# An attention and convolution kernel: whole products gathered in every other region, conv steps between them

## The chip, the cores and the metric

The kernel runs on one core of a Trainium2 chip. The metric is the time on the device from start to end in microseconds (us), median of three runs: 3374.07 us before the change (3363.94 to 3385.05).

## The reference, cut to what matters

Two layers on four images of 128 channels and 128 x 128 pixels, in float32.

Layer 0 is region attention with a conv network behind it:

```python
reg = x[:, :, ih, iw]                       # 9 x 9 regions of 16 x 16 pixels, step 14, so 2 overlap
tok = reg as (b * 81, 256, 128)
q, k, v = split(layernorm(tok) @ w_qkv)     # 4 heads of 32 channels
o = softmax(q k^T / sqrt(32)) v             # per region and head, 256 x 256
tok = o @ w_out + b_out + tok
xf = (sum of the regions' tok at each pixel) / (how many regions hold the pixel)
ym = layernorm(xf) @ w_p0 + b_p0            # 256 channels
ym = depthwise_conv_5x5(ym)
ym = gelu(gelu(batchnorm(ym)))              # means over all images
x1 = ym @ w_p2 + b_p2 + xf
```

Layer 1 quantises to 4 bits, convolves 3 x 3, normalises over the batch, twice, and adds x1. It is the last part of the kernel, and the change does not touch it, except for the preparation of its two quantised weights, which runs beside the attention.

## The kernel before, in words

Channels lie on the 128 partitions. An image is cut into nine **bands** of one row of nine regions each, so there are T = 36 bands, and the main loop runs over bands t and over the nine regions j of a band. The first stage (attention and depthwise conv) ends at about 2434 us, then come `gelu_stage` and `last_stages`.

**Region work.** For each region the loop calls `scores(j)` (L663: eight matmuls in tiles of 32 rows by 128 columns, one per head and half of the keys, then two exponentials of 128 x 1024 on ScalarE), the value step of the region before (`last`, made of `values(j)`, L725: products of 128 rows by 32 columns, then the sums over the keys with a matrix of ones, then on VectorE a reciprocal and two multiplications, and on GpSimd the addition at the seam), `halves(j)` (L679: the two halves of the keys are added, one pair on GpSimd and one on VectorE) and `values_in(j)` (L653: v of the region, two whole 128 x 128 products and a copy on ScalarE).

**Side work.** Between these calls stand three lists of side steps, which `beside(t)` (L765) returns for each region. They hold
- `one`: layer norm and projection of the next band, in two chunks `a1` and `a2` of nine steps: squares, variance (matmuls with ones, tiles of 128 x 32), deviation, spread (the row of factors goes through DRAM and comes back on all partitions), second (scaling), and four q and k products of 512 or 384 columns;
- `two`: the band before, in two chunks `b1` and `b2` of eleven steps: two output projections (`wo`, L499), squares, variance, deviation, spread, second, and four products with `w_p0` (L515) whose results go to DRAM as `y2_d`;
- `conv`: steps taken from the list `todo`.

**The list todo.** It first holds the quantisation of layer 1's weights (`quantised`, L281) and the making of the conv matrices (`band_matrices`, L202, whose `turn`, L253, reorders a 40 x 2048 tile on VectorE or ScalarE). Later it gets the depthwise conv of each finished image (`conv_steps`, L545): one first step that loads, then 32 tiles per image, each with loads of u and w from DRAM, 24 matmuls in tiles of 40 rows by 32 columns, two copies on ScalarE, statistics on VectorE and stores to `cv_d` in pieces of 256 bytes. The last image is cut into a half and two quarters of 16 tiles each. `share` says how many steps a band takes, and a fixed order (0, 3, 5, 7, 1, 2, 8, 4, 6) which regions get them.

**What sets the order.** On TensorE, ScalarE, VectorE and SyncE (`MANUAL`) instructions stand in the order in which the code emits them; every engine works its queue in that order. Nearly all DMAs are issued from SyncE's queue, and a store is issued right after the step that made it (`run` and `flush`).

**Buffers.** The score tiles take four of the eight PSUM banks (one buffer of two tiles), the value tile one (`ps_o`), and three banks (`ps_m`, "pm") serve everything else: value inputs, statistics, products, conv steps. In SBUF: `xp` holds the input rows (3), `xfp` the output projection (1), `xnp` the scaled rows (3), `y2p` two buffers per half for the y stores, `attn_t` the small attention tiles and v (3).

**The tail.** After band 36 the region pools are closed, `beside(T)` gives the post chain of the last band with conv steps of the third unit between, and the last quarter image runs with all its weights in SBUF (`all_w`), loaded from GpSimd's queue.

## Time and profile before

| what | us |
|---|---|
| time, median of three runs | 3374.07 |
| span of the profiled execution | 3381.3 |
| start, to the first scores | 35.4 |
| band 0 | 52.5 |
| bands 1 to 9 (no conv steps; the matrices are made) | 501.0 |
| bands 10 to 27 (conv of images 0 and 1) | 1080.6 |
| bands 28 to 32 (conv of image 2) | 376.1 |
| bands 33 and 34 (conv of a half of image 3) | 170.6 |
| band 35 and the tail | 217.9 |
| gelu and last stages | 946.9 |

A stretch ends where the scores of the next band start, read from the start times of the score matmuls, nine regions to a band. The mean granted TensorE clock over the span is 0.960 of full speed. Busy times of TensorE take in modelled ends of pipelined matmuls, so 93% busy does not mean 93% of its peak; distances between starts are the safer measure. A float32 matmul of the program stands as two records in the trace.

### The profile page before, as it was taken

To read this page: it belongs to the slowest core of one execution; us is meant where nothing else is said; L and a number is where in the kernel's file an instruction comes from. 1 tells how busy PE (TensorE), PEld (TensorE's weight loads), DVE (VectorE), ACT (ScalarE), POOL (GpSimd) and SP (SyncE) were. 2 spreads that over 40 slices of the span, in tenths; PEclk is the share of its full clock that TensorE was granted. 3 is DMA by queue.
4 is the path that set the end of the run, shared out by engine and by line. 5 is a ranking of instruction groups with operands and counts; after the bars stand their busy time and mean duration, and the time that the engine had idled before them with its cause. 6 is when DMAs were issued, how large, how long until landed. Compare 5 with 4: busy or idle time off the path is not lost. (4 is left out here: it accounts for less than half of the span.)

```text
span 3381.3 us, 75962 instructions
## 1 busy us (share of the span) xinstructions
PE 3144.9 (93%) x30922; PEld 1584.0 (47%) x30922; DVE 2006.5 (59%) x3229; ACT 2006.7 (59%) x2818; POOL 841.9 (25%) x1060
## 2 busy tenths in 40 slices
PE   6999889999999999999999999984799999999998
PEld 3555445555454554554444445552544444444343
DVE  4767666766766666666655555551455555666543
ACT  4677667666666666666655556551267677433433
POOL 2443334333333333333322222220011111000000
PEclk8999989999999999999999999896599999999999
DMA  2455655788887788878699988877699999552298
GB/s 89 131 155 148 157 137 142 185 195 190 190 199 178 184 181 195 195 189 194 157 203 206 203 193 191 206 188 198 175 360 359 359 356 316 166 174 81 77 358 312
DMA packets 812012, 682.64 MB, mean 202 GB/s; under 512 B 581550, under 2 KB 696327, under 8 KB 811655
## 3 DMA queue, kind: packets, MB, share of 16 engines
q1 hardware_dynamic: 792071, 669.03, 72.8%
q10 hardware_dynamic: 18560, 4.72, 0.6%
q8 instruction: 247, 4.05, 0.5%
q0 software_dynamic: 1024, 3.93, 0.4%
q14 instruction: 110, 0.90, 0.1%
HBM read 410.68 MB, written 270.81 MB: 202 GB/s over the span
## 5 line engine op out<-in xcount | busy, mean ns | idle before, releaser
L751 DVE RECIPROCAL rd<-po 128x256 f32<-128x256 f32 x324 | 569.4, 1757 | 513.5 <-PE po L739 511.3
L1023 PE MATMUL pc<-q,wq 128*128 128x512 fp8e4 x3168 | 702.0, 381 | 14.4 <-DVE q L1035 14.4
L676 ACT ACTIVATE pt<-sc 128x1024 f32<-128x1024 f32 x648 | 626.2, 1019 | 96.5 <-PE sc L668 64.2
L686 POOL TENSOR_TENSOR sm<-pt 128x512 f32<-128x512 f32 x324 | 417.7, 1289 | 1064.3 <-ACT pt L676 629.7
L1023 PEld LDWEIGHTS <-wq 128*128 128x128 fp8e4 x3168 | 309.1, 98 | 417.6 <-issue 50.0
L600 PE MATMUL pm<-u,w 40*32 40x504 f32 (+5 forms) x7680 | 370.9, 497 | 48.3 <-DMA u<-y_d 33.2
L668 PE MATMUL sc<-q,kr 32*128 32x256 f32 x5184 | 402.4, 405 | 1.9 <-ACT pt L676 1.7
L731 PE MATMUL po<-pt,v 128*32 128x256 f32 x5184 | 349.9, 388 | 26.8 <-ACT v L660 16.7
L611 DVE BATCH_NORM_STATS2 st<-c 128x6 f32<-128x512 f32 (+2 forms) x384 | 175.4, 506 | 255.5 <-ACT c L607 254.7
L668 PEld LDWEIGHTS sc<-q,kr 32*128 32x128 f32 x5184 | 247.8, 185 | 150.3 <-issue 105.1
L607 ACT COPY c<-pm 128x512 f32<-128x512 f32 (+1 forms) x256 | 132.4, 562 | 288.9 <-PE pm L600 247.3
L446 PE MATMUL pm<-xn,wqkv 128*128 128x512 f32 (+1 forms) x576 | 270.2, 594 | 29.1 <-DVE xn L376 26.8
L515 PE MATMUL pm<-xn,wp 128*128 128x512 f32 (+1 forms) x576 | 259.7, 575 | 8.0 <-DVE xn L376 7.8
L656 PEld LDWEIGHTS pm<-wqkv,yr 128*128 128x128 f32 x1296 | 183.4, 194 | 177.5 <-issue 100.6
L600 PEld LDWEIGHTS pm<-u,w 40*32 40x32 f32 x7680 | 161.3, 110 | 218.4 <-issue 139.6
L1081 PE MATMUL pb<-cv,wp 128*128 128x512 f32 x512 | 232.6, 598 | 12.2 <-ACT cv L1072 12.2
L686 DVE TENSOR_TENSOR sm<-pt 128x512 f32<-128x512 f32 x324 | 228.2, 704 | 11.9 <-ACT pt L676 11.9
L520 ACT ACTIVATE y<-pm,bp 128x512 f32<-128x512 f32 (+1 forms) x288 | 180.5, 640 | 80.2 <-PE pm L515 73.8
L731 PEld LDWEIGHTS po<-pt,v 128*32 128x32 f32 x5184 | 137.1, 109 | 193.8 <-issue 47.8
L656 PE MATMUL pm<-wqkv,yr 128*128 128x128 f32 x1296 | 221.1, 294 | 1.8 <-DVE rstd L352 1.1
L739 PE MATMUL po<-sm,ones 128*32 128x256 f32 x2592 | 201.6, 381 | 8.0 <-POOL sm L686 8.0
L1031 DVE BATCH_NORM_STATS2 st<-pc 128x6 f32<-128x512 f32 x256 | 165.6, 689 | 67.3 <-PE pc L1023 67.3
(149 smaller groups left out, 3468.0 us busy)
## 6 DMA issues: line engine op xcount, KB each, us to landing
cv<-cv_d SPq DMA_DIRECT2D x64, 1024.0 KB
u<-y_d SPq DMA_DIRECT2D x224, 256.0 KB
cv_d<-c SPq DMA_DIRECT2D x192, 256.0 KB
xn<-row SPq DMA_DIRECT2D x80, 512.0 KB
y_d<-y SPq DMA_DIRECT2D x160, 256.0 KB
xfl<-xf_d SPq DMA_DIRECT2D x64, 512.0 KB
id_d<-y SPq DMA_DIRECT2D x64, 512.0 KB
idt<-id_d SPq DMA_DIRECT2D x64, 512.0 KB
```

The costliest lines, as they stand in the source:

```text
L446: nc.tensor.matmul(pm[:, : n * P], wqkv[:, m * P : (m + 1) * P], held["xn"][hh], start=True, stop=True,)
L515: nc.tensor.matmul(pm[:, : n * P], wp0[:, h, :], held["xn"][hh], start=True, stop=True)
L600: nc.tensor.matmul(pc[half][32 * q : 32 * q + 32, j, :, a:z], wt[hs, s, c0 + c, :], ut[hs, :, c, a + s - 1 : z + s - 1], start=(s == 1), s ...
L656: nc.tensor.matmul(pv[:, c, :], region(yr, j)[:, c * P : (c + 1) * P], wqkv[:, 2 * P :], start=True, stop=True)
L668: nc.tensor.matmul(sc[h // 2][:, h % 2, kc, :].rearrange("p (r c) -> p r c", c=RS), region(kr, j)[hs, kc * P : (kc + 1) * P], queries(j, h ...
L676: nc.scalar.activation(pt, sc[p], AF.Exp)
L686: add(sm, pt[:, :, 0, :], pt[:, :, 1, :], ALU.add)
L731: nc.tensor.matmul(po[hs, 0, :], v[:, kc, hs], pt[h // 2][:, h % 2, kc, :], start=(kc == 0), stop=(kc == 1),)
L739: nc.tensor.matmul(po[hs, 1, :], ones, sm[h // 2][:, h % 2, :], start=True, stop=True)
L751: nc.vector.reciprocal(rd, po[:, 1, :])
L1023: nc.tensor.matmul(pc[:, h], w[:, t, :], q1[b][:, r + dy : r + dy + RB, dx : dx + P], start=(t == 0), stop=(t == 8),)
L1081: nc.tensor.matmul(pb[:, m], wp2[:, h, :], cv[:, h, px], start=(h == 0), stop=(h == 1))
```

## The change

- **Regions.** `beside(t)` returns four lists per region. From band 10 on, all whole products (q, k, output projection, `w_p0`) stand in the even regions, together with the value inputs, and conv steps stand in the odd regions first (order 1, 3, 5, 7, 8, 4, 6, 2, 0). Up to band 9 the whole products are spread over all nine regions. The purpose is to change between whole products and tiled matmuls less often, and to give the regions more even work.
- **Values of two regions at once.** `values_in` runs in even regions and fills a tile for regions j and j + 1, with one copy on ScalarE.
- **A projection one band later.** The second half's `w_p0` steps (`b2[7:]`) are kept in `left` and run in the next band's first region. The first squares of a band's input run at the end of the band before (`early`).
- **Matrix steps.** `turn` is split into two halves, all on VectorE; the edges and rows of the matrices are single steps, one per region. The largest weight is found by a store, a load onto all partitions and a reduction in place of GpSimd's `partition_all_reduce`.
- **Shares.** The steps of an image are spread evenly over the bands left for it. The third unit (a quarter of image 3) runs wholly in band 35, up to two steps per region.
- **Tail.** Half the weights are loaded ahead, half beside the first four conv steps, from SyncE's queue; no conv step stands inside the last band's chain.
- **Buffers.** `xp` 3 to 2, `xfp` 1 to 2, `attn_t` 3 to 2, and a pool `attn_v` of 2 for the value inputs.

```diff
-        work, dev, xnp, xfp = pool("work", 1), pool("dev", 2), pool("xnp", 3), pool("xfp", 1)
+        work, dev, xnp, xfp = pool("work", 1), pool("dev", 2), pool("xnp", 3), pool("xfp", 2)
...
-        xp, yp, sums = pool("xp", 3), pool("yp", 2), pool("sums", 1)
-        att, attn_t = pool("att", 2 if safe else 4), pool("attn_t", 2 if safe else 3)
+        xp, yp, sums = pool("xp", 2), pool("yp", 2), pool("sums", 1)
+        att, attn_t, attn_v = pool("att", 2 if safe else 4), pool("attn_t", 2), pool("attn_v", 2)
...
-            def turn(c, s):
-                by_c = scratch(32 * 64)[:KD]
-                copy = nc.scalar.copy if s % 2 else nc.vector.tensor_copy
-                copy(by_c.rearrange("p (c m) -> p m c", m=32), held.pop((c, s)))
-                nc.sync.dma_start(
-                    out=dw_d[c // 16 : (c + 64) // 16, :, s, :].rearrange("k p n -> p k n"),
-                    in_=by_c.rearrange("p (k n) -> p k n", n=16 * 32),
-                )
+            def turn(c, s, half):
+                if half == 0:
+                    held["c"] = scratch(32 * 64)[:KD]
+                by_m, by_c = held[c, s], held["c"]
+                nc.vector.tensor_copy(
+                    by_c[:, half * 1024 : half * 1024 + 1024].rearrange("p (c m) -> p m c", m=32),
+                    by_m[:, :, 32 * half : 32 * half + 32],
+                )
+                if half:
+                    del held[c, s]
+                    nc.sync.dma_start(
+                        out=dw_d[c // 16 : (c + 64) // 16, :, s, :].rearrange("k p n -> p k n"),
+                        in_=by_c.rearrange("p (k n) -> p k n", n=16 * 32),
+                    )
             def several(*steps):
                 def run_all():
...
             pieces = [(c, s) for c in range(0, 2 * P, 64) for s in range(3)]
-            steps = [several(zeros, *each(edges, [(b,) for b in range(B)])), padded_taps]
-            for n in range(0, GR, 2):
-                steps.append(several(*each(by_outputs, [(ro,) for ro in range(n, n + 2)])))
-            steps += [lambda: None]
-
-            for n in range(0, len(pieces) + 2, 2):
+            steps = [zeros, *each(edges, [(b,) for b in range(B)]), padded_taps, lambda: None]
+            steps += each(by_outputs, [(ro,) for ro in range(GR)])
+            steps += [lambda: None, lambda: load(*pieces[0])]
+
+            for n, p in enumerate(pieces):
                 steps.append(
-                    several(*each(turn, pieces[max(n - 2, 0) : n]), *each(load, pieces[n : n + 2]))
-                )
+                    several(lambda p=p: turn(*p, 0), *each(load, pieces[n + 1 : n + 2]))
+                )
+                steps.append(lambda p=p: turn(*p, 1))
             return steps
         def quantised(n, w):
...
-                am = small.tile([P, 1], F32, name="am")
+                am = small.tile([P, 1], F32, name="am", bufs=2)
-                held["alpha"] = small.tile([P, 1], F32, name="alpha")
-                nc.gpsimd.partition_all_reduce(held["alpha"], am, P, bass_isa.ReduceOp.max)
+                held["row"] = row = rowp.tile([4, 256], F32, name="row")
+                store(row[0:1, :P].rearrange("a p -> p a"), am)
...
+
+            def spread():
+                row = held["row"]
+                held["am"] = dev.tile([P, 256], F32, name="rstd")[:, :P]
+                nc.sync.dma_start(out=held["am"], in_=bass.AP(row.tensor, row.offset, [[0, P], [1, P]]))
             def scales():
-                alpha = held["alpha"]
...
-                        room = tail[0] if tail and at else xfp
-                        held["xf"] = room.tile([P, LB * P], F32, name="xf")
+                        held["xf"] = xfp.tile([P, LB * P], F32, name="xf")
...
             def values_in(j):
-                pv = ps_m.tile([P, 2, P], F32, name="pm")
-                for c in range(2):
-                    nc.tensor.matmul(
-                        pv[:, c, :], region(yr, j)[:, c * P : (c + 1) * P], wqkv[:, 2 * P :], start=True, stop=True
-                    )
-                v = attn_t.tile([P, 2, P], F32, name="v")
-                nc.scalar.copy(v, pv)
-                S["v", j] = v
+
+                two = range(j, min(j + 2, NR))
+                pv = ps_m.tile([P, 2, 2, P], F32, name="pm")
+                for m in range(len(two)):
+                    for c in range(2):
+                        nc.tensor.matmul(
+                            pv[:, m, c, :], region(yr, j + m)[:, c * P : (c + 1) * P], wqkv[:, 2 * P :],
+                            start=True, stop=True,
+                        )
+                v = attn_v.tile([P, 2, 2, P], F32, name="v")
+                nc.scalar.copy(v[:, : len(two)], pv[:, : len(two)])
+                for m in range(len(two)):
+                    S["v", j + m] = v[:, m]
             def scores(j):
                 sc = [ps_s.tile([P, 2, 2, NT], F32, name=f"sc{p}") for p in range(2)]
...
-            one = ln1_chunks(t + 1) if t + 1 < T else []
+            one = list(early) if t else ln1_chunks(1)
+            early[:] = ln1_chunks(t + 2) if t + 2 < T else []
             two = post_chunks(t - 1) if t else []
+            had = len(todo)
             if t >= 2:
                 b, i = bands[t - 2]
                 if i == NR - 1 and b < B - 1:
                     todo.extend(conv_steps(b))
-                    share[0] = -(-len(todo) // (NR if b < B - 2 else 5))
+                    share[0] = NR if b < B - 2 else 5
                 elif b == B - 1 and i == 4:
                     todo.extend(conv_steps(B - 1))
-                    share[0] = NR
+                    share[0] = 2
                 elif b == B - 1 and i == 6:
                     todo.extend(conv_steps(B))
-            conv = [todo.pop(0) for _ in range(min(share[0], len(todo)))]
+                    share[0] = 1
+
+            fresh = len(todo) > had
+            n = len(todo) // share[0] if fresh else -(-len(todo) // max(share[0], 1))
+            conv = [todo.pop(0) for _ in range(n)]
+            share[0] -= 1
             a1, a2 = one if one else ([None] * 9,) * 2
             b1, b2 = two if two else ([None] * 11,) * 2
             if t == T:
-                c = conv + [None] * (9 - len(conv))
                 return [
-                    *b1[:2], *b2[:2], b1[2], b1[3], b2[2], b2[3], b1[4], b2[4], *c[:3], b1[5], b2[5],
-                    *c[3:6], b1[6], *b1[7:], b2[6], *b2[7:], *c[6:],
+                    *conv, *left, *b1[:2], *b2[:2], b1[2], b1[3], b2[2], b2[3], b1[4], b2[4], b1[5], b2[5],
+                    b1[6], *b1[7:], b2[6], *b2[7:],
                 ]
+
             c = [[] for _ in range(NR)]
-            for j in sorted((0, 3, 5, 7, 1, 2, 8, 4, 6)[: len(conv)]):
+            d = [[] for _ in range(NR)]
+            twice = len(conv) > NR
+            for j in sorted((1, 3, 5, 7, 8, 4, 6, 2, 0)[: len(conv)]):
                 c[j] = [conv.pop(0)]
+                d[j] = [conv.pop(0)] if twice and j and conv else []
             x1 = lambda: fetch(t, 0)
             x2 = lambda: fetch(t, 1)
-            return [
-                ([], [a1[0], *c[0]], []),
-                ([a1[1]], [b1[0], b1[1], *c[1]], [a1[2], b1[2]]),
-                ([b1[3]], [a1[3], *c[2]], [b1[4], a2[0]]),
-                ([a2[1]], [b1[5], *c[3]], [a1[4], a2[2]]),
-                ([], [b1[6], a2[3], a1[5], a1[6], *c[4]], [b2[0], b2[1], b2[2]]),
-                ([b2[3]], [a1[7], a1[8], *c[5]], [b2[4], a2[4], b1[7], b1[8]]),
-                ([], [b2[5], b1[9], b1[10], *c[6]], [a2[5], a2[6]]),
-                ([], [b2[6], x1, a2[7], a2[8]], c[7]),
-                ([], [x2, b2[7], b2[8], *c[8]], [b2[9], b2[10]]),
+            f, left[:] = list(left), b2[7:]
+            s1 = early[0][0] if early else None
+            plan = [
+                ([a1[1]], [], f, [*c[0], a1[2]]),
+                ([], [a1[3], *c[1]], [], [a2[0]]),
+                ([a2[1]], [a1[4]], b1[:2], [*c[2], a2[2]]),
+                ([], [a2[3], *c[3]], [], [b1[2]]),
+                ([b1[3]], [a2[4]], [*a1[5:], *b2[:2]], [*c[4], b1[4]]),
+                ([], [b1[5], *c[5]], [], [b2[2]]),
+                ([b2[3]], [b1[6]], a2[5:], [*c[6], b2[4]]),
+                ([], [b2[5], x1, *c[7]], [], []),
+                ([], [b2[6], x2], b1[7:], [*c[8], s1]),
             ]
+            if t == 0:
+                plan[0] = ([], [], [], [*c[0], *a1[:3]])
+            if t <= NR:
+
+                left[:] = [*b1[9:], *b2[7:]]
+                full = (f[:3], f[3:], b1[:2], a1[5:7], a1[7:], b2[:2], a2[5:7], a2[7:], b1[7:9])
+                plan = [(one, two, w, four) for (one, two, three, four), w in zip(plan, full)]
+            return [(one, two, three, four + d[j]) for j, (one, two, three, four) in enumerate(plan)]
         def run(steps):
             for s in steps:
...
-        todo, share = [], [3]
+        todo, share, left, early = [], [0], [], []
-        for pair in zip(quantised(0, w1), quantised(1, w2)):
-            todo.append(lambda pair=pair: [s() for s in pair])
+        one, two = quantised(0, w1), quantised(1, w2)
+        for n in range(len(one) + 1):
+            todo += one[n : n + 1] + two[max(n - 1, 0) : n]
+        share[0] = NR + 1
...
                     run(side[1])
-                    values_in(j)
+                    if j % 2 == 0:
+                        values_in(j)
                     run(side[2])
+                    run(side[3])
                     last = lambda j=j, values=values: values(j)
             last()
             post_begin(T - 1)
...
             tail += [actx.enter_context(tc.tile_pool(name=f"late{n}_{tag}", bufs=n)) for n in (1, 4)]
-            all_w = []
-            for n, s in enumerate(beside(T)):
-                if len(all_w) < NCK:
-                    all_w.append(tail[0].tile([P, 3, 16, 32], F32, name=f"w{n}"))
-                    weights(all_w[n], n, 0, 2, nc.gpsimd.dma_start)
-                run([s])
+            all_w = [tail[0].tile([P, 3, 16, 32], F32, name=f"w{k}") for k in range(NCK)]
+            for k in range(NCK // 2):
+                weights(all_w[k], k, 0, 2, nc.sync.dma_start)
+            run(beside(T))
             flush(len(stores))
             run(todo)
-            for s in conv_steps(len(units) - 1, 4, (all_w, tail[1])):
+            for n, s in enumerate(conv_steps(len(units) - 1, 4, (all_w, tail[1]))):
                 s()
                 flush(len(stores), nc.scalar)
+                if n < NCK // 2:
+                    weights(all_w[NCK // 2 + n], NCK // 2 + n, 0, 2, nc.sync.dma_start)
+            flush(len(stores))
     def affine(mean, var, n, gamma, beta, name):
```

More of the change, by code (lines that the diff above doesn't have):

```diff
@@ L296, in largest @@
             def largest():
-                am = small.tile([P, 1], F32, name="am")
+                am = small.tile([P, 1], F32, name="am", bufs=2)
                 nc.vector.tensor_reduce(am, held["w"], AX.X, ALU.max, apply_absolute_value=True)
-                held["alpha"] = small.tile([P, 1], F32, name="alpha")
-                nc.gpsimd.partition_all_reduce(held["alpha"], am, P, bass_isa.ReduceOp.max)
+                held["row"] = row = rowp.tile([4, 256], F32, name="row")
[4 more added lines that the diff above has]
+                nc.sync.dma_start(out=held["am"], in_=bass.AP(row.tensor, row.offset, [[0, P], [1, P]]))
             def scales():
-                alpha = held["alpha"]
+                alpha = held["alpha"] = small.tile([P, 1], F32, name="alpha", bufs=2)
+                nc.vector.tensor_reduce(alpha, held["am"], AX.X, ALU.max)
                 nc.vector.tensor_scalar(alpha, alpha, 1e-12, None, ALU.add)
                 nc.vector.tensor_scalar(ks, alpha, 1.0 / 105.0, None, ALU.mult)
-                held["ra"] = small.tile([P, 1], F32, name="ra")
+                held["ra"] = small.tile([P, 1], F32, name="ra", bufs=2)
                 nc.vector.reciprocal(held["ra"], alpha)
@@ L325, in clip_all @@
                 clip()
-            return [load, largest, clip_all, widen, to_int, to_f8]
+            return [load, largest, spread, clip_all, widen, to_int, to_f8]
         def normalise(src, n):
```

## The prediction

> **What bounds the kernel now.** I read the page's busy line first, then the busy time of seven stretches, then TensorE in order of time, then the waits. The seven stretches are the start with band 0, bands 1 to 9, 10 to 27, 28 to 32, 33 and 34, band 35 with the tail, and the two later stages. A band's edge is every ninth start of a group of score matmuls (L668). The columns are length, busy time of each engine, granted TensorE clock, DMA share, GB/s.
>
> ```profile
> PE 3144.9 (93%) x30922; PEld 1584.0 (47%) x30922; DVE 2006.5 (59%) x3229; ACT 2006.7 (59%) x2818; POOL 841.9 (25%) x1060
> ```
>
> ```profile
> 35.40:87.90 52.50, 40.07 (x423) 22.50 (x422) 30.46 (x55) 29.46 (x43) 18.49 (x24) 0.90 0.16 54
> 87.90:588.90 501.00, 456.06 (x4501) 246.60 (x4500) 340.84 (x513) 350.76 (x536) 197.76 (x241) 0.97 0.54 146
> 588.90:1669.50 1080.60, 1060.04 (x12077) 541.93 (x12076) 725.61 (x1118) 737.29 (x1190) 374.93 (x476) 1.00 0.80 188
> 1669.50:2045.60 376.10, 349.66 (x4037) 165.66 (x4036) 217.11 (x339) 221.91 (x359) 102.97 (x133) 0.96 0.90 198
> 2045.60:2216.20 170.60, 156.81 (x2537) 90.67 (x2536) 92.46 (x174) 91.98 (x151) 40.69 (x51) 0.93 0.87 202
> 2216.20:2434.10 217.90, 147.03 (x3617) 101.48 (x3616) 84.52 (x283) 61.31 (x125) 30.92 (x50) 0.69 0.71 181
> 2434.10:3381.00 946.90, 915.00 (x3680) 406.70 (x3680) 508.61 (x726) 503.51 (x401) 70.82 (x75) 0.99 0.76 265
> ```
>
> TensorE sets the time up to band 27. From band 28 the DMA share of 0.90 makes it a joint bound, and in the tail the clock falls to 0.69. The last row is not touched by the change. TensorE in time order, band 12:
>
> ```profile
> 726.53 1.07 PE L731 MATMUL po<-pt,v 128*32 128x256 f32 x16
> 727.42 0.61 PE L739 MATMUL po<-sm,ones 128*32 128x256 f32 x8
> 727.85 0.51 PE L345 MATMUL pm<-xt,ones 128*32 128x192 f32 x8
> 728.92 0.53 PE L345 MATMUL pm<-sq,ones 128*32 128x192 f32 x8 [0.56 <-ACT sq L339]
> 729.38 2.78 PE L600 MATMUL pm<-u,w 40*32 40x512 f32 x48
> ```
>
> Ends are modelled, so I use starts alone. A value product (L656) that stands among other whole products takes 0.44 us from its start to the next start (693.84 to 694.28). Alone between a conv step and the scores it takes 0.64 (653.09 to 653.73). **The 0.20 is the price of one more group of whole products.** The same reading gives per region: scores 1.08, values and sums (L731, L739) 1.43, a conv step of 24 instructions 2.71 to 2.92, a 512-column product 0.86, a 384-column one 0.64, statistics (L345) 0.86 or 0.64. The shape of the waits is in these lines, a stretch of band 6 on ScalarE and then band 0 on TensorE:
>
> ```profile
> 356.13 3.67 ACT L256 COPY u<-u 40x2048 f32<-40x2048 f32 x1 [3.33 <-DVE u L256]
> ```
>
> ```profile
> 69.95 1.08 PE L739 MATMUL po<-sm,ones 128*32 128x256 f32 x8 [7.97 <-POOL sm L686]
> ```
>
> **What the Trainium skill says.** "TensorEngine Tiling (Array Packing)", section Key Properties: changing the tiling mode, not just the tile, drains TensorE. The trace agrees: scores (32x128 tiles) to values (128x32) start 0.30 us after the last score against about 0.20 within a group. "TensorE: Matmul & The Clock Gate", The mechanism: a weight load overlaps running matmuls only in other row groups; so a whole product after a switch shows its load, 0.53 instead of 0.43 for the first 512-column pass. The same page, What's actually happening: an idle window of some 3.4 us halves the clock; bands 6 and 7, with gaps of 7 us, show 0.90 and 0.87. "DMA: Bandwidth & Descriptors", Issuing engines are not separate DMA queues: another issuing queue saves only issue time. So moving the tail's weight loads from GpSimd's queue to SyncE's buys no bandwidth; no run here shows it yet.
>
> **The change, part by part.**
>
> Switches. In the order in which each program hands matmuls to TensorE, I counted changes of tiling between scores, values-and-statistics, whole products and conv steps: 1144 before, 995 after. All of the difference is entries into whole products, 368 against 219. 149 x 0.20 = 30 us, on the path in bands 10 to 27, partly hidden by transfers later. A full conv band goes from ten groups of whole products to five.
>
> Band sums, all by start-to-start durations. Nine regions 9 x 2.51 = 22.6, statistics 3.0, nine values 4.0, ten 512- and ten 384-column products 15.0: together 44.6. A band without conv adds nine groups x 0.20 = 46.4, before and after alike (bands up to 9 keep products in every region). A conv band adds 4 steps, 11.1, and ten groups, 2.0: 57.7. It takes 60.9, so 3.2 is waiting; a band without conv takes 51.3 and waits 4.9. After, five groups and four steps at 2.82 give 56.9.
>
> Waits. They sit in short regions: bands 3 to 5 have regions of 3.1, 4.2, 4.4 us beside ones of 7 and 8. A region needs 2.04 us of exponentials (two of 1019 ns, one score buffer), and on VectorE 1.76 + 0.39 + 0.18 + 0.70 = 3.03. The new plan, added up the same way, gives bands up to 9 regions of 4.0 to 6.8 and conv bands 5.3 to 9.1. ScalarE's sum per conv band is about 44 us, VectorE's 43, both under 57. Statistics follow their squares by a region that holds a conv step, 2.1 to 2.3 us of ScalarE queue against 2.8 us of scores and values. In the region with the first output projections VectorE needs 6.5 against 6.0 on TensorE; three result buffers take that up. I keep 0.5 us of waits per band, and 0.8 for each region with neither products nor conv (three per image).
>
> Bands 1 to 9: 9 x (46.4 + 1) = 427, plus 8 for 24 half turns of about 1 us on VectorE (half of L256's 1951 ns) where four 3.69 us copies stood on ScalarE ahead of the exponentials: 435 for 501, so -66, of which 33 is bands 6 and 7 alone (69.2 and 67.6). Bands 10 to 27: per image 9 x 45.6 + 32 x 2.82 = 501, plus 8 of waits; twice 1018 for 1081, -62. Band 0: the all-reduce on GpSimd is replaced by a small store and load, so the 7.97 us wait goes, and some of the ragged regions: -11.
>
> Bands 28 to 34, the same transfers: DMA busy 0.90 x 376 = 338 and 0.87 x 171 = 148. TensorE's own sum is 318 and 137. With both near full I take 362 and 160: -14 and -10. Lower bound, DMA at 0.97: 349 and 153. Upper bound: as now.
>
> Band 35 and tail: band 35 takes all 17 steps of its quarter image (16 of about 1.7 us, DMA 3 us each) and grows from 65 to 85; then the chain of the last band runs with no conv between. Before it took 82 us (2272 to 2354), because conv steps stood inside it, with lines such as this one:
>
> ```profile
> 2307.71 0.65 PE L600 MATMUL pm<-u,w 40*32 40x128 f32 x8 [9.54 <-DMA u<-y_d]
> ```
>
> Without them it is 6 us for the last seam, 5 for the projection, 3 for statistics, 2 x 4 for the two DMA hops, 10 for the scale and products, 4 for the store: about 36 to 40. The last 16 steps keep their 80, plus some 4 for half the weights now loaded beside them. 85 + 38 + 84 = 207 for 218: -12.
>
> Costed at nothing: one value copy of 128x512 (589 ns) for two of 128x256 (380 each) saves 0.17 us on ScalarE, which has slack; input buffers 3 to 2 (the new load is issued when its tile is freed, four regions ahead of use); two buffers for the projection; second halves of the projection (p0) a band later, whose first readers, the conv loads, stand behind their stores in the same SyncE queue. **Added waits:** each conv step now stands directly ahead of the next region's scores, so a late tile delays the scores, the exponentials and VectorE's reciprocal; eight y stores come within two regions and reuse two buffers per half after about 7 us, where a store's way is some 4 us: ScalarE waits if SyncE's queue is late, with the exponentials behind it.
>
> Sum: -11 - 66 - 62 - 14 - 10 - 12 = -175; 3374 - 175 = 3199, forecast 3200.
>
> **The rivals.** A, the sum above. B, waits move rather than vanish: only switches (30), band 0 (11), the turns (33) and the tail (12) are gained: 3374 - 86 = 3288. For it: VectorE at 75% and xn tiles one region after their issue; against: no region of the plan asks more of ScalarE than of TensorE. C, transfers hide fully: bands 28 to the end of the tail at DMA 0.97, (338 + 148 + 155) / 0.97 = 661 for 765, so -104 instead of -36: 3131. Against: the tail's waits are latency, not bandwidth. D, slower: six products in one region need three result buffers, so evictions of 0.65 us queue behind the 2.04 us of exponentials. Three products beyond the buffers hold in each of five regions would cost about 1.4 us a region: 7 us x 26 conv bands = +182, without the 62 and 24 gained there; 3374 + 182 - 66 - 11 - 12 = 3467. Against: a product takes 0.86 on TensorE, longer than its eviction.
>
> **How the numbers follow.** A 0.66, B 0.18, C 0.07, D 0.09. The range 3130 to 3315 holds A to C with the bounds of the transfer-bound bands; D and a little of B's edge lie outside. Faster by over 1% is A, B and C less a little: 0.88; within 1%: 0.03; slower: 0.09.
>
> **What would show it.** Right: bands 3 to 5 at about 47.5 us, 12 to 16 at 57 to 58, bands 6 and 7 within 3 us of their neighbours, no 8 us wait in band 0, the last scores to the last stage's first transfer about 122 us. Wrong: waits of scores (L684 in the new file) for exponentials or of conv steps for u in bands 11 to 16; ScalarE waiting for y stores; bands 28 to 34 no shorter than now. The prediction fails above all if the regular waits come back elsewhere.

## The result and the profile after

The changed kernel takes 3293.09 us (median of four runs, 3282.93 to 3295.39) against 3377.59 us for the kernel before on the same chip. The ratio is 0.9747 (95% interval 0.9717 to 0.9777), so 84 us are gained where 175 were forecast.

The changed kernel in stretches; columns as before: length, busy time of each engine, granted TensorE clock, DMA share, GB/s.

```profile
33.10:75.10 42.00, 38.22 (x421) 21.63 (x420) 28.31 (x45) 29.01 (x39) 18.47 (x23) 0.96 0.42 94
75.10:518.30 443.20, 431.73 (x4492) 228.50 (x4491) 351.81 (x538) 328.36 (x489) 192.51 (x240) 1.00 0.59 161
518.30:1561.30 1043.00, 1028.73 (x12078) 515.73 (x12077) 726.99 (x1123) 744.24 (x1120) 374.70 (x477) 1.00 0.82 195
1561.30:1930.50 369.20, 343.29 (x4037) 164.01 (x4036) 218.83 (x338) 221.13 (x338) 103.71 (x133) 0.95 0.89 201
1930.50:2104.70 174.20, 160.64 (x2548) 89.95 (x2540) 92.33 (x170) 91.85 (x143) 40.88 (x51) 0.88 0.84 194
2104.70:2342.30 237.60, 157.98 (x3627) 106.87 (x3624) 86.70 (x289) 63.44 (x125) 21.83 (x33) 0.69 0.67 175
```

| stretch | before | forecast | after | missed by |
|---|---|---|---|---|
| band 0 | 52.5 | 41.5 | 42.0 | 0.5 |
| bands 1 to 9 | 501.0 | 435 | 443.2 | 8 |
| bands 10 to 27 | 1080.6 | 1018 | 1043.0 | 25 |
| bands 28 to 32 | 376.1 | 362 | 369.2 | 7 |
| bands 33 and 34 | 170.6 | 160 | 174.2 | 14 |
| band 35 and the tail | 217.9 | 207 | 237.6 | 31 |

The misses come to 85 us; bands 10 to 27 and the tail make two thirds of them. Bands 3 to 5 take 48.2 to 48.9 us (forecast 47.5), bands 11 to 16 57.3 to 58.4 (57 to 58), bands 6 and 7 are like their neighbours (49.4, 49.0), and the 8 us wait of band 0 is gone. The last two stretches got longer than before the change. In one group of the page ScalarE now waits for a buffer; before the change this group waited for TensorE. The group before, then after:

```profile
L520 ACT ACTIVATE y<-pm,bp 128x512 f32<-128x512 f32 (+1 forms) x288 | 180.5, 640 | 80.2 <-PE pm L515 73.8
L531 ACT ACTIVATE y<-pm,bp 128x512 f32<-128x512 f32 (+1 forms) x288 | 183.0, 641 | 146.1 <-DMA y_d<-y 80.3
```

The last numbers are the idle time ahead of the group, after the change 146.1 us, of which 80.3 ended with the landing of a store of y. Of these 80.3, bands 10 to 27 have 23.6 in 36 waits, bands 28 to 32 have 41.7 in 16. In band 29, SyncE's, ScalarE's and TensorE's lines of one such wait (start, length, engine and line):

```profile
1625.75 5.12 SPq L412 DMA_DIRECT2D xr<-in_x_dram  x1
1630.96 3.41 SPq L398 DMA_DIRECT2D y_d<-y  x3
1635.39 0.58 ACT L531 ACTIVATE y<-pm,bp 128x384 f32<-128x384 f32 x1 [3.04 <-DMA y_d<-y]
1636.03 1.40 PE L526 MATMUL pm<-xn,wp 128*128 128x384 f32 x2 [2.06 <-ACT y L531]
```

The y tiles were written from 1622.03 on, but SyncE issued their stores at 1630.96, behind conv tiles and an input load that held it 5 us. ScalarE waited for the buffer, TensorE for ScalarE, and the exponentials behind that eviction came late too.

### The profile page after: what moved, and what is told of

Its sections match the earlier page's. It is cut to its first block, busy times and chain, and to the rows that moved or that the text cites. A ratio compares the mean times of both kernels' runs of the same rounds, so it can differ in the third digit from the quotient of the medians.

```text
span 3289.0 us, 75777 instructions
## 1 busy us (share of the span) xinstructions
PE 3093.5 (94%) x30922; PEld 1541.3 (47%) x30922; DVE 2020.6 (61%) x3247; ACT 1992.0 (61%) x2670; POOL 828.3 (25%) x1042
## 4 chain that ended last, share of the span: by engine, by line
PE 77%; DMA 10%; ACT 5%; DVE 3%; SPq 2%; issue 2%; ACTq 0%; POOL 0%; DVEq 0%; POOLq 0%
PE pc L1064 19%; PE pm L611 9%; PE sc L684 9%; PE po L747 8%; PE pm L458 6%; PE pb L1122 6%; PE pm L526 5%; PE pm L670 4%; PE po L755 4%; DMA y_d<-y 3%; PE pm L510 3%; PE pm L357 3%; DMA xn<-row 2%; DMA cv_d<-c 2%; DMA u<-y_d 2%
## 5 line engine op out<-in xcount | busy, mean ns | idle before, releaser
L1064 PEld LDWEIGHTS <-wq 128*128 128x128 fp8e4 x3168 | 309.0, 98 | 417.7 <-issue 50.2
L747 PE MATMUL po<-pt,v 128*32 128x256 f32 x5184 | 361.5, 398 | 8.7 <-DVE part L771 7.7
L526 PE MATMUL pm<-xn,wp 128*128 128x512 f32 (+1 forms) x576 | 249.7, 565 | 37.2 <-ACT y L531 20.0
L531 ACT ACTIVATE y<-pm,bp 128x512 f32<-128x512 f32 (+1 forms) x288 | 183.0, 641 | 146.1 <-DMA y_d<-y 80.3
L458 PE MATMUL pm<-xn,wqkv 128*128 128x512 f32 (+1 forms) x576 | 251.5, 565 | 11.6 <-DVE xn L388 9.0
L702 DVE TENSOR_TENSOR sm<-pt 128x512 f32<-128x512 f32 x324 | 243.5, 751 | 29.7 <-ACT pt L692 29.5
L611 PEld LDWEIGHTS pm<-u,w 40*32 40x32 f32 x7680 | 145.2, 112 | 216.8 <-issue 161.4
L670 PE MATMUL pm<-wqkv,yr 128*128 128x128 f32 x1296 | 193.4, 290 | 0.0
L670 PEld LDWEIGHTS pm<-wqkv,yr 128*128 128x128 f32 x1296 | 159.0, 192 | 68.7 <-issue 44.4
```

Source lines behind the costliest of these rows:

```text
L458: nc.tensor.matmul(pm[:, : n * P], wqkv[:, m * P : (m + 1) * P], held["xn"][hh], start=True, stop=True,)
L526: nc.tensor.matmul(pm[:, : n * P], wp0[:, h, :], held["xn"][hh], start=True, stop=True)
L611: nc.tensor.matmul(pc[half][32 * q : 32 * q + 32, j, :, a:z], wt[hs, s, c0 + c, :], ut[hs, :, c, a + s - 1 : z + s - 1], start=(s == 1), s ...
L670: nc.tensor.matmul(pv[:, m, c, :], region(yr, j + m)[:, c * P : (c + 1) * P], wqkv[:, 2 * P :], start=True, stop=True,)
L702: add(sm, pt[:, :, 0, :], pt[:, :, 1, :], ALU.add)
L747: nc.tensor.matmul(po[hs, 0, :], v[:, kc, hs], pt[h // 2][:, h % 2, kc, :], start=(kc == 0), stop=(kc == 1),)
```

## The experiments

Kernels are built on the changed one unless the text says before. Ratios are to the kernel before, with 95% intervals; the changed one has 0.9747.

**Products in every region.** Is a switch worth 0.20 us?

```diff
-            if t <= NR:
+            if t <= 3 * NR:
```

(and the last product kept back from the band before stands early in region 1, so that conv loads stand behind the y stores they read)

> The changed kernel with the whole products spread over every region also in bands 10 to 27 (four more entries into whole products a band, 72 in all), all else kept. Theory S (a switch costs 0.20 us on the path): bands 11 to 16 and 20 to 25 grow by 0.8 us each, bands 10 to 27 by 14 us, the whole to about 3307. Rival W (the even spread removes waits, of ScalarE for y stores above all, which the gathering made): the waits of y in bands 10 to 27 fall from 24 us to under 5, and the bands stay within 0.3 us of now, the whole within 5 us of 3293.

3308.86 us, 0.9801 (0.9784 to 0.9817). Bands 11 to 16 take 58.6 on average where the changed kernel takes 57.75: 0.22 for each of the four entries. Bands 10 to 27 grow by 11 us; the rest of the 16 lies in later bands, which the edit leaves alone and which differ by some us from run to run. Theory S holds. ScalarE's waits for y stores in bands 10 to 27 did fall as rival W says, from 23.6 to 1.5 us, but the bands grew all the same. Since the edit took these waits away, 0.22 is rather low: against the 57.3 of bands without such waits (seven y tiles, next) an entry costs some 0.3.

**Seven y tiles.** Are the y waits what is missing?

```diff
-        y2t = [[y2p.tile(... y2_{h}{n}) for n in range(2)] for h in range(2)]
+        y2t = [y2p.tile(... y2_{n}) for n in range(7)]
```

(paid for by one tile fewer for the exponentials and one fewer for the value inputs)

> The changed kernel with seven y tiles in one ring instead of two per half (four in all), paid for by one pt tile and one v tile fewer. Theory W (waits for y stores): ScalarE's waits of y for its store fall from 80 us to under 20, the first regions of bands 29 to 34 from 10 to 15 us to about 8, bands 28 to 34 from 543 us to about 515, and the whole by some 30 us to 3263. Theory T (the transfers set bands 28 to 34): the y waits fall but waits for u tiles or rows take their place, bands 28 to 34 stay within 6 us, and the whole stays within 8 us of 3293. If the pt tile given up matters, every band of 10 to 27 grows by some 0.2 us a region, 30 us in all.

3304.66 us, 0.9788 (0.9764 to 0.9812): no gain, and by the medians 12 us slower, though the two intervals touch. Bands 11 to 16 are 57.3 each, so theory W holds there, for 7.5 us in bands 10 to 27. But bands 4 and 5 take 52 to 53 where the changed kernel takes 49, and bands 28 to 34 take 556 where it takes 543 (552 in a kernel with the same code up to band 34, the one with the quarter image split). ScalarE hardly waits for y stores any more (10 us in all); VectorE waits for a row, TensorE for VectorE, in band 30:

```profile
1729.24 1.29 DVE L388 TENSOR_TENSOR xn<-xn,xt 128x512 f32<-128x512 f32 x2 [6.78 <-DMA xn<-row]
1731.25 5.29 PE L611 MATMUL pm<-u,w 40*32 40x512 f32 x40 [5.28 <-DVE xf L511]
```

The wait was handed on, as theory T says; but the bands did not stay within its 6 us, and its reason, that the transfers set these bands, is at most a part (see the small stores).

**Three input tiles.**

```diff
-        xp, yp, sums = pool("xp", 2), ...
+        xp, yp, sums = pool("xp", 3), ...
```

(paid for like the seven y tiles)

> The changed kernel with three input tiles x as before the change instead of two, paid for by one pt tile and one v tile fewer (bands of the run with more y tiles show that these two cost nothing). My prediction put the third tile at nothing. Theory Q (with two tiles SyncE stands at the input load until VectorE has scaled xn, with y stores and rows behind it): SyncE's waits for xn fall from 227 us to under 40, ScalarE's waits for y stores from 80 to under 50, the bands of 10 to 27 by 0.3 us each, the whole by 8 to 15 us. Theory N: SyncE has slack there, and the whole stays within 4 us.

3295.82 us, 0.9755 (0.9739 to 0.9771). SyncE's waits for xn go from 227 to 1 us, and nothing is gained: theory N. That two input tiles cost nothing is right, if the two tiles given up for the third cost nothing either; bands 11 to 16 with seven y tiles, at 57.3, speak for that.

**Scaling later.** b2[6], the scaling of the second chunk's rows, goes from region 8 to region 0 of the next band.

```diff
-            f, left[:] = list(left), b2[7:]
+            f, left[:] = list(left), b2[6:]
```

> The changed kernel with the scaling of the second rows (xn of chunk b2) moved from the last region of a band to the first of the next, from band 10 on. Theory X (the row load has only a short region to land in when region 7 has no conv step): bands 17, 18, 26 and 27 fall from 57.1 to about 55, bands 10 and 19 from 60.4 to about 57, the waits of VectorE for xn rows in bands 10 to 27 from 14 us to under 4, the whole by about 15 us. Theory N (that wait lies beside ScalarE's or TensorE's own work): the wait goes, the bands stay within 0.5 us, and the whole within 4 us.

3391.54 us, 1.0051 (1.0034 to 1.0068): 98 us slower than the changed kernel; both theories fail. Region 0 of a conv band grows from some 7.8 to 11.9, because its products now wait for a scaling that stands behind all of the region's work on VectorE. Band 12, region 0, TensorE and VectorE:

```profile
661.25 1.16 PE L670 MATMUL pm<-wqkv,yr 128*128 128x128 f32 x8
664.54 1.38 DVE L388 TENSOR_TENSOR xn<-xn,xf 128x384 f32<-128x384 f32 x2
665.39 4.51 PE L526 MATMUL pm<-xn,wp 128*128 128x384 f32 x8 [2.98 <-issue]
```

The first of the two scalings ends as the products start (the profile names no releaser here; the times do). A step moved off a wait is not free when its reader stands in the same region.

**The quarter image split.** 9 of its 17 conv steps in band 35, 8 in the last chain, in the chain's order of before.

```diff
-                    share[0] = 1
+                    share[0] = 2
```

> The changed kernel with the 17 steps of the next to last quarter image shared again between band 35 and the chain of the last band, 9 and 8, the chain's order as before the change. Theory S (two tiles ahead are too few for 17 steps in one band): band 35 falls from 114 us to about 75, the chain grows from 44 to about 75, the stretch from band 35 to the last stage's first transfer falls from 237.6 us to about 222, the whole by 15 us. Theory L (the tail is a sum of latencies wherever the steps stand): what band 35 loses the chain gains, and the stretch stays within 5 us.

3281.68 us, 0.9718 (0.9695 to 0.9741). This interval touches that of the changed kernel, so the gain is read from the stretch. Band 35 up to its last value products, in the changed kernel and in this one, then the rest of this one up to the last stages:

```profile
2104.70:2218.30 113.60, 88.25 (x1991) 55.93 (x1988) 46.34 (x113) 40.08 (x71) 17.20 (x20) 0.77 0.68 177
2113.80:2172.10 58.30, 53.38 (x1128) 32.81 (x1124) 37.37 (x75) 33.72 (x53) 17.25 (x20) 0.97 0.73 194
2172.10:2341.00 168.90, 97.37 (x2506) 70.75 (x2500) 49.08 (x214) 29.62 (x72) 3.63 (x10) 0.58 0.68 177
```

227.2 against 237.6: band 35 loses 55 us, and the rest, 124.0 in the changed kernel, takes back 45. Theory S in sign, two thirds of its size. Other runs agree on band 35: 109 to 118 us in all seven with the whole quarter image there, 54 to 59 in all five that split it.

**Matrix steps alone, on the kernel before.**

```diff
-        todo, share = [], [3]
+        todo, share = [], [7]
```

(with the changed `turn`, `band_matrices` and `quantised`)

> The kernel before with only the matrix steps of the change: half turns on VectorE, single small steps, seven a band, and the largest value spread by a store and a load instead of GpSimd's all-reduce. My prediction gives this part 11 us in band 0 and 33 us in bands 6 and 7: bands 6 and 7 at about 52, the whole 44 us faster than before, 3334. A rival says that the half turns delay VectorE's reciprocals in bands 5 to 8 as the full ones delayed the exponentials: then half of it, 3355. A second rival says that the wait in band 0 was covered: 33 us.

3364.47 us, 0.9966 (0.9953 to 0.9978). Band 0 falls to 40.2, as forecast. Bands 6 and 7 fall to 51.8 and 52.0, 33 us together, as forecast too. But bands 4 and 5 rise to 66.8 and 67.5 and take 32 us back. It looks as if the long bands had moved, but these are two different waits. That of bands 6 and 7 is TensorE's for a copy of value inputs, which stands on ScalarE behind a long copy of the matrices. It stays when nothing but the row stores is moved (the kernel before with row stores by GpSimd, below; its band 6, ScalarE, then TensorE):

```profile
345.51 3.67 ACT L256 COPY u<-u 40x2048 f32<-40x2048 f32 x1 [3.34 <-DVE u L256]
349.44 1.93 PE L731 MATMUL po<-pt,v 128*32 128x256 f32 x16 [7.02 <-ACT v L660]
```

That of bands 4 and 5 is new. Band 4 of the run with the matrix steps, SyncE, then its wait, then VectorE:

```profile
229.66 18.60 SPq L398 DMA_DIRECT2D y_d<-y  x3
```

```profile
SPq L398 <- DMA row<-rstd: 17.4, 2, 12.3
```

```profile
265.63 1.29 DVE L388 TENSOR_TENSOR xn<-xn,xt 128x512 f32<-128x512 f32 x2 [14.67 <-DMA xn<-row]
```

The y tiles were ready at 230.1. Their last two stores started at 242.41 and 247.90, 1.7 and 1.6 us after ScalarE had issued a row store (240.75 and 246.26). In the trace the transfers of both queues share eight completion semaphores, and each of the two y stores has that of the row store ahead of it. That the semaphores are the reason is argued from this; no run changed their number. SyncE then issued the loads of rows only at 256.32 and 258.27, and VectorE stood 15 us.

**Row stores by GpSimd,** with the changed kernel, with the matrix steps, and alone on the kernel before.

```diff
-                nc.scalar.dma_start(out=row[:, :w], in_=rstd[0:P:32, :])
+                nc.gpsimd.dma_start(out=row[:, :w], in_=rstd[0:P:32, :])
```

> The changed kernel with the small stores of row (rstd to memory) issued by GpSimd instead of ScalarE, so that they no longer take turns with SyncE's transfers on the same completion semaphores. Theory C (SyncE's stores and u loads wait for row stores only because they share those semaphores): SyncE's waits of stores and u loads for row fall from 105 us to under 10, ScalarE's waits for y stores from 80 us to under 40, bands 28 to 34 from 543 us to about 520, the whole to about 3270. Rival G (GpSimd's own queue delays the rows): xn comes later, VectorE's waits for xn grow, each band of 1 to 27 by 1 us or more, the whole above 3315. Rival N: the waits only change their name, and the whole stays within 8 us of 3293.

> The kernel before with the matrix steps of the change alone (the earlier run, in which the long bands 6 and 7 turned into long bands 4 and 5), and now the row stores issued by GpSimd. Theory C (in bands 4 and 5 SyncE stood 12 us at a y store for a row store of ScalarE, because the two take turns on one completion semaphore, and VectorE then 15 us for the row): bands 4 and 5 fall from 67 to about 52, and the whole from 3364 to about 3335, which is the 44 us that my prediction gave the matrix steps. Rival: the transfers of the matrix steps themselves are what is waited for; then bands 4 and 5 stay above 60, and the whole above 3355.

> The kernel before with nothing but the row stores issued by GpSimd. The matrix steps with the same edit took 104 us off, the matrix steps alone 12. Theory C (the two meet only in bands 4 to 7; the rest of the gain is the rows' own, in every stage): bands 10 to 27 at 1057, 28 to 32 at about 353, bands 6 and 7 still long, in all 60 us faster than before, about 3317. Rival: both are needed everywhere, and the rows alone give less than 20 us.

On the changed kernel 3291.26 us, 0.9743 (0.9727 to 0.9759): rival N. With the matrix steps 3273.50, 0.9691 (0.9673 to 0.9709), which is less than the changed kernel takes, without its plan. Alone 3320.51, 0.9815 (0.9796 to 0.9834), as theory C says; bands 6 and 7 stay long there, 70.7 and 66.4. Bands 4 and 5 with matrix steps: 50.2 and 49.8. Full conv bands fall from 60.9 to 59.5, and bands 28 to 32 from 376 to 353 (the run with matrix steps):

```profile
1589.70:1942.90 353.20, 339.23 (x4041) 163.61 (x4040) 216.97 (x339) 219.61 (x359) 112.16 (x153) 0.99 0.97 211
```

**Row stores by SyncE,** on the kernel before and with the matrix steps (`nc.sync` in the same line).

> The kernel before with the row stores issued by SyncE. Rows by GpSimd gave 62 us. Theory I (what is saved is ScalarE's issue of four row stores a band, some 0.5 us each ahead of exponentials): any other queue gives it, and this run comes to about 3320. Theory C (SyncE's queue must not wait for a row at all): here SyncE meets each row store in its own order and waits for ScalarE's rstd there, so only the issue time is saved, 1.4 us in each full conv band, and the rest is not: bands 28 to 32 stay at 368 or more, the whole at 3345 to 3365.

> The matrix steps alone with the row stores issued by SyncE. Theory I: as with rows by GpSimd, bands 4 and 5 at 50, the whole at 3275. Theory C: bands 4 and 5 still wait, at 55 or more if SyncE stands at the row store with x loads and band matrices behind it, and the whole at 3320 or more.

3327.45 us, 0.9855 (0.9831 to 0.9879), and 3281.89, 0.9722 (0.9697 to 0.9746): three quarters of what GpSimd's queue gives, or nine tenths. Full conv bands take 59.3, bands 4 and 5 50.7 and 49.8. SyncE now waits for rstd (the factors that the row store takes), 361 us in the run without the matrix steps, and it costs little. Theory C as I put it falls, theory I holds for the larger part. Either move takes away two things at once, ScalarE's issue and SyncE's wait for a row store of ScalarE that comes later in the order of work; no run parts them. In band 12 of the kernel before the issue is plain to see:

```profile
727.50 0.48 ACTq L362 DMA_DIRECT2D row<-rstd  x1
728.03 0.84 ACT L339 ACTIVATE sq<-xt 128x768 f32<-128x768 f32 x1 [0.56 <-ACT rstd L360]
```

The squares start 0.5 us late, and TensorE's statistics at 728.92, a line of my own prediction, wait 0.56 for them. Four such issues are 1.9 us a band, and a full conv band lost 1.6. All 144 make some 70 us of ScalarE that no busy time counts. The rest of GpSimd's gain lies in bands 28 to 34, where SyncE takes 534 us and GpSimd 520.

**Small stores.**

```diff
-    [2 * P * GR * P, ng] ... cv[:, j]
+    [2 * P * GR * P, 1 if n == 2 else ng] ... cv[:, j, :1] if n == 2 else cv[:, j]
```

(and the next stage reads image 1's result in place of image 2's)

> The changed kernel in which the stores of image 2's convolution (bands 28 to 32) carry one row group in eight: as many store instructions on the same queue, in the same places, with an eighth of the bytes. The other seven eighths of that image's convolution result are left out, and the next stage reads image 1's in their place. Theory T (the bytes bound bands 28 to 32, so that TensorE's saved time there counts for nothing): 14.7 of some 74 MB go, the bands fall from 369 us (365 to 381 in four runs of near kinds) to about 335, TensorE's own 318 with some waits. Rival L (the order of the queue and its waits bound them, whatever the bytes): they stay above 360.

3272.64 us, 0.9686 (0.9670 to 0.9703). Bands 28 to 32:

```profile
1557.90:1911.80 353.90, 338.16 (x4037) 163.73 (x4036) 217.29 (x338) 220.79 (x338) 103.69 (x133) 0.95 0.76 171
```

15 us less at a DMA share of 0.76: between the two theories. Bytes are a part; even with room on the DMA engines these bands stay some 36 us above the prediction's 318 for TensorE's own work.

**Combinations.**

> The changed kernel with the quarter image shared between band 35 and the last chain, and the row stores by GpSimd: both edits that came out no slower alone. If they act in different stretches, 11 us and 2 us add up, and the whole comes to 3280. If the chain of the last band gains too, because its rows and its tiles no longer share semaphores, 3272. If GpSimd's issue adds to each of the chain's four hops, 3288.

3276.91 us, 0.9713 (0.9691 to 0.9734): the split alone, within the noise. ScalarE's waits for y stores stay, 93 us for 95.

> The changed kernel with seven y tiles, the row stores by GpSimd, and the quarter image shared with the last chain. Alone the three gave +11, -2 and -11 us. If the plan of the change can use both freed queues and tiles (theory Q: with two y tiles a half ScalarE waits, with rows on ScalarE the queue waits, so either alone only hands the wait on): bands 11 to 27 at 57.3, bands 28 to 32 at about 350 with a transfer share over 0.95, the whole about 3245. If the y stores bunched in two regions are the trouble by their bytes (theory B): bands 28 to 34 stay at 535 or more, the whole at 3280.

3274.30 us, 0.9679 (0.9662 to 0.9696). With tiles and queue freed, bands 11 to 16 are at 57.3 to 57.5, but bands 28 to 34 take 541, as theory B says. Its reason, the bytes, isn't shown: the DMA share there is 0.91 and 0.88, below the 0.97 above.

For the last two, which keep the split and the rows by GpSimd, `beside` returns the lists of the kernel before from band 28 on:

```diff
+            if t > 3 * NR:
+                left[:] = []
+                plan = [
+                    ([], [*f, *c[0]], [], []),
+                    ([a1[1]], [b1[0], b1[1], *c[1]], [a1[2], b1[2]], []),
...
+                    ([], [x2, b2[7], b2[8], *c[8]], [b2[9], b2[10]], [s1]),
+                ]
```

> The changed kernel up to band 27, and from band 28 the order of steps of the kernel before (products in every region, second p0 halves in their own band, two y stores to a region), with the quarter image shared as before and the row stores by GpSimd. Theory B (the plan's eight y stores in two regions are what bands 28 to 34 pay for): these seven bands take about 518 us as in the run of before with matrix steps and rows by GpSimd, ScalarE's waits for y stores there go to under 5 us, and the whole is about 3245. Theory Q (queue and tiles, not the plan): they stay at 535 or more, the whole above 3265.

> The same with seven y tiles as well, which in bands 10 to 27 meet the plan's bunched y stores: those bands fall from some 58.5 with rows by GpSimd to 57.3 each, 15 to 20 us, and the whole to about 3228, faster than the kernel before, the changed one and every run so far. If the tiles cost what they gain, as in the run with seven tiles alone: 3245.

3280.67 us, 0.9693 (0.9677 to 0.9709), and with seven y tiles 3250.98, 0.9597 (0.9580 to 0.9614). Bands 28 to 34 take 525 and 528 where theory B said 518, and ScalarE's waits for y stores are gone there, so it holds in the main. The edit puts back the whole order of these bands, conv steps too; that the bunched y stores are the part that costs is argued. Rows by GpSimd cost the plan something in bands 10 to 27: 1060 with no other edit and 1071 here, for 1043, with ScalarE's waits for y stores at 35 and 48 us, for 24. With seven tiles these bands take 1043 again. That last run is the fastest of all. Its bands 10 to 27, 28 to 32, 33 and 34:

```profile
516.60:1559.50 1042.90, 1031.85 (x12081) 517.68 (x12080) 721.92 (x1124) 748.32 (x1120) 407.64 (x549) 0.99 0.84 195
1559.50:1923.70 364.20, 345.57 (x4047) 163.56 (x4046) 218.04 (x340) 224.19 (x343) 113.96 (x153) 0.97 0.96 208
1923.70:2087.70 164.00, 151.17 (x2537) 86.80 (x2536) 91.60 (x174) 92.03 (x143) 45.14 (x59) 0.94 0.93 212
```

## Why the prediction was wrong

The sign was right; half of the size was not there. The step that failed is the account of waits: 0.5 us a band in bands 10 to 27, nothing for the new order of bands 28 to 34 with its eight y stores in two regions, and nothing for tiles that come late in band 35. They were short by 25, 21 and 29 us. By the steps of the prediction:

- **Switches, 30 us:** right where it was tried, in bands 10 to 27. Put back, they cost 0.22 to 0.3 each. The Trainium skill, "TensorEngine Tiling (Array Packing)", Key Properties, says that a change of tiling mode drains TensorE, and a price of this kind agrees. One reading beside it is wrong: the 0.53 us of a first 512-column pass is no sign of a switch, since in the same trace it also stands after value products, where the tiling doesn't change (44 passes). The price doesn't rest on it.
- **Band 0, -11:** right, -10.5, and -12.3 with the matrix steps alone.
- **Bands 1 to 9, -66:** -58. The half that lies in bands 6 and 7 was right in size and in reason ("four 3.69 us copies stood on ScalarE ahead of the exponentials"): these two bands lose 33 us with the matrix steps alone and 38 in the changed kernel. What the prediction did not see is that the same steps, with ScalarE's row stores, put a wait of 15 us into each of bands 4 and 5 of the kernel before. The new plan has no wait of SyncE for a row above 7.3 us in bands 1 to 9, and row stores on either other queue take it away too. The missing 8 us are spread: 49.2 a band for 48.3.
- **Bands 10 to 27, -62:** -37.6. "I keep 0.5 us of waits per band" is what failed, and with it the 0.8 for a region with neither products nor conv. Full bands take 57.8 for 57.4, and seven y tiles give that back. Bands 17, 18, 26 and 27 take 57.1 for some 55.4, bands 10 and 19 take 60.2 and 60.6 for some 55 and 53 by the same sum: 12 x 0.4 + 4 x 1.7 + 5.2 + 7.3 = 24 of the 25. In these six bands region 7 has no conv step and takes 3.1, and region 8 takes back 1 us (in band 19 five), waiting for the row that the step would have hidden; that this is all of it is argued, not shown. (Band 19 took 57.1 in the run with the quarter image split, whose code is the same there, so 3.5 us of it come and go.)
- **Bands 28 to 34, -24:** -3.3, less than kernels with the same code there differ by (543 to 552). "With both near full I take 362 and 160" failed. The DMA share of 0.90 was no bound: with rows by GpSimd and the old plan it is 0.97 in bands 28 to 32, and these seven bands take 518. The old plan lost 27 us to its row stores (547 to 520 with nothing else moved). The new one loses time to its own order: with rows moved and seven y tiles these bands take 541, with rows moved and the old order put back 525. The eight y stores in two regions, which I had named as an added wait and costed at nothing, make ScalarE wait 51 us for y stores here. With rows moved and seven tiles that falls to 6, and TensorE waits for rows (through VectorE, 19 us) and for u (10 us) instead. That these come late because they queue behind the bunched stores is likely; no run moved the stores alone.
- **Band 35 and tail, -12:** +20. "Band 35 ... grows from 65 to 85" is the wrong term: it takes 113.6. Its conv tiles wait for u, 17.8 us of TensorE in all, first behind y stores of its own region 0, which the later second halves brought about (TensorE's first tiles in band 35, then the scores of two of its regions):

```profile
2123.67 3.50 PE L611 MATMUL pm<-u,w 40*32 40x128 f32 x104 [7.98 <-DMA u<-y_d]
2130.15 2.09 PE L684 MATMUL sc<-q,kr 32*128 32x256 f32 x16
2151.61 1.15 PE L684 MATMUL sc<-q,kr 32*128 32x256 f32 x16
```

The same scores take 2.09 us in some regions and 1.15 in others. The granted clock over band 35 is 0.77, against 0.95 before the change and 0.97 with the quarter image split, where no tile waits for u. The prediction priced its 16 conv tiles at 1.7 us each, as if the clock stayed up. That the waits bring the clock down fits these runs; it was not tried apart.

The chain takes 45 (forecast 38) and the last steps 79 (84). The chain before took 74 by the same edges; the prediction's 82 begin 9 us earlier, inside its 65 for band 35, and 207 for 218 is -11, not -12. Steps put back in the chain return 10 us; why the rest stays, two tiles ahead being too few or the transfers, was not tried.

Rival B, "waits move rather than vanish", gave 3288 and the run 3293. Its sum is right by luck: it counted 33 us in bands 1 to 9, where 58 were gained, and 12 in the tail, where 20 were lost.

## What to carry to other kernels

A wait that is counted away by engine sums can come back where a queue in order, a pool of two buffers and a full stretch meet; for each buffer that a new order fills faster, write down when its store will be issued, not when it could be. When one remedy gives nothing, look which wait took its place, and try the two together: here seven y tiles alone gave 0.9788 and the other three edits 0.9693, against 0.9747 without any, and all together 0.9597. When a wait goes and another of its size turns up, look at what each waits for before you call it the same one: the long bands 4 and 5 here were not the long bands 6 and 7. Look at the issuing instructions on a compute engine's queue: they count as no busy time, and they stand ahead of its work.

## What the runs showed of the hardware

- A row store issued by ScalarE holds its queue 0.48 us (median of 144). The same 144 issues on SyncE's queue or GpSimd's (614 ns each) made the kernel before 1.5 and 1.9% faster, 49 and 62 us. "DMA: Bandwidth & Descriptors", Issuing engines are not separate DMA queues, in the Trainium skill, calls the issue time usually small next to the transfer. It is small here too, where a row store of GpSimd's takes 2.8 or 4.4 us from issue to landing; but on ScalarE it stands ahead of work of like size, such as squares of 0.84 us.
- Bands 28 to 32 and 33 to 34 of the kernel before ran at DMA shares of 0.90 and 0.87, and with the row stores on GpSimd's queue and the matrix steps changed, which leaves their bytes as they were, at 0.97 and 0.91.
